# Attention without padded query and key products: a four-layer block kernel on one core

## Chip, cores, metric

The kernel runs on one core of a Trainium2 chip. A core has a matrix engine (TensorE; PE in the profile, its weight loads PEld), a vector engine (VectorE, DVE), a scalar engine (ScalarE, ACT), a general engine (GpSimd, POOL) and a queue engine (SyncE, SP), and 16 DMA engines that they share. Each engine works through its own instructions in order, and waits for others by semaphores. The matrix engine writes to PSUM, which has eight banks of 128 x 512 floats. DMAs here are issued from SP and from POOL. The metric is the device time of one launch, in microseconds.

## What is computed

Four layers stand behind each other on x of shape (4, 512, 288) in float32, with one condition vector per batch. Layers 0, 1 and 3 are transformer blocks with 16 heads of 18 features; layer 0's feed-forward part picks 2 of 4 experts for every token; layer 2 rotates x in a subspace of 64 dimensions. Cut down (n is a normalization, sh, sc and g come from the condition):

```python
h = n(x) * (1 + sc_msa) + sh_msa
q, k, v = split(h @ w_qkv + b_qkv)                 # 16 heads of 18 features
att = softmax(einsum("bhqd,bhkd->bhqk", q, k) * 18 ** -0.5)
x = x + g_msa * (einsum("bhqk,bhkd->bqhd", att, v) @ w_proj + b_proj)
h = n(x) * (1 + sc_mlp) + sh_mlp
x = x + g_mlp * (gelu(h @ w1 + b1) @ w2 + b2)      # layer 0: weighted sum over two experts
# layer 2: U = qr(P).Q; R = expm(skew(silu(cond) @ W.T + b)); x = x + ((x @ U) @ R - x @ U) @ U.T
```

## The kernel before

**Order.** The program is emitted in Python in the order in which the work is wanted, and a scheduler places the instructions of each engine; helpers pin the order where it matters. `mm` (L75) chains nearly all matmuls in program order. `take`, `beside_of` and `in_turn` (L95 to L105) keep, for an engine, the last instruction to which others are tied: `beside_of` puts an instruction behind it, `in_turn` also makes it the new last one.

**Stages.** In the profiled execution attention 0 runs to about 415 us, the experts to 931, attention 1 to 1303, the feed-forward part of layer 1 to 1485, the rotation and attention 3 to 1866, and layer 3's feed-forward part to the end. Side jobs (`tick`, L770) run through all of them: the Householder reflections of layer 2 (`reflections`, L577), the matrix exponential (`exponential`, L652), the modulation of the next layers (`modulation`, L320).

**Attention** (L776). A group r is four heads g of one batch b; there are 16 groups a layer. The four heads lie in the four quarters of the 128 partitions, each 18 features and 14 rows of padding, so that four products of 32 rows can run beside each other. `queries_and_keys(r)` (L829) projects the 128 padded rows of q and of k for 512 tokens: per side one product of the 32 features left over and two of 128 features, in halves of 256 tokens, into two `de` banks, from which ACT writes the tiles `qk0` and `qk1` with the bias (L856). The bias puts 1.0 into row 18 of every key head.

A group has 8 quads (`quad`, L888): k counts half a tile of 128 tokens, and a quad is two `row_max` (L862) and two `weight` (L875). `row_max` multiplies q by k to a 128 x 512 score tile, from which DVE takes the maximum of every row (L873). After the eighth quad `shift` (L913) transposes these maxima and subtracts them from the q tile, in row 18 of each head. So `weight`, which runs nine quads later with keys as rows, gets scores minus maximum, which ACT exponentiates (L885). `sums` (L898) multiplies the weights by the values, whose ones column gives the denominator; `collect` (L943) and `invert` (L964) move sums, denominators and reciprocals by DMAs on POOL and SP.

Between quads `work_off` (L1092) runs pieces of jobs by the letters of a table (L1042 to L1064): Q is the projection of group r + 1, A the transposed input of the next batch, X values or output projection, R the routing of the experts (L1717). Steps (L1039) stand at fixed quads: `invert(r - 2)` at k = 4, the sums at k = 1 and 5.

**PSUM.** One bank `av`, four `sc` (scores and hidden features), three `de` (all else), L64.

**Weights.** q and k weights come padded to 32 columns a head from the host (`_layout`, L2074): 288 x 1024 floats, loaded into `wqk` and `wqkr` (L241, L254). x of batches 1 to 3 is loaded tile by tile in 12 DMAs (L2025).

Of the kernel before, what the change touches and what calls it, by code (L numbers as in the profile page):

```python
# [16 lines left out]
P = 128  # L17
# [6 lines left out]
HC = P // D  # L24
OR = 64
# [3 lines left out]
E = 4  # L29
# [14 lines left out]
def kernel(ctx: ExitStack, tc: tile.TileContext, a: dict, out: bass.AP):  # L44
# [19 lines left out]
    banks = {"sc": 4, "de": 3}  # L64
# [4 lines left out]
    def misc(name):  # L69
        return bank("de", name)  # L70

# [21 lines left out]
    queues = {nc.sync: "SP", nc.scalar: "ACT"}  # L93
# [56 lines left out]


# [19 lines left out]
    def load_x(b):  # L171
        for t in range(NT):
            nc.sync.dma_start(x[:, b * NT + t, :], a["x"][b, t * P : (t + 1) * P, :])

# [62 lines left out]

    def attention_weights(l):

        w = {}  # L240
        w["qk"] = wt.tile([P, MC, 2 * NG * P], F32, tag="wqk", name=f"wqk{l}")  # L241
        w["qkr"] = wt.tile([2 * RR, NG * P], F32, tag="wqkr", name=f"wqkr{l}")
# [3 lines left out]
        w["bqk"] = wt.tile([P, 2 * NG], F32, tag="bqk", name=f"bqk{l}")  # L246
# [7 lines left out]
        def qk():  # L254
            load(w["bqk"], a[f"bqk{l}"])
            full_chunks(w["qk"], a[f"wqk{l}"])
# [6 lines left out]
        def qk_rest():  # L263
            for s in range(2):
                remainder(w["qkr"], a[f"wqk{l}"][:, :, s * NG * P : (s + 1) * NG * P], [s])

        def projection(g):
# [4 lines left out]
        return w, [  # L272
            qk,
            qk_rest,
# [41 lines left out]
    dram = ctx.enter_context(tc.tile_pool(name="dram", bufs=1, space=bass.MemoryType.DRAM))  # L316
# [3 lines left out]
    def modulation(l):  # L320
# [14 lines left out]
        def half(i):  # L335
# [25 lines left out]
            ps = misc(f"psada{l}_{i}")  # L361

            def products(ns):
                for kc in range(KC):
                    for n in ns:
                        q = (n + 1) % 3
                        nc.tensor.matmul(
                            ps[q * RR : (q + 1) * RR, 0:C],
                            lhsT=siluT[:, kc, :],
                            rhs=pieces[n][:, kc, :],  # L370
                            start=(kc == 0),
                            stop=(kc == KC - 1),
                        )

            def gated():
                nc.vector.tensor_add(gate[:, i, :], gate[:, i, :], ps[0:B, 0:C])
# [4 lines left out]
            if (l, i) in by_rows:  # L381
                for q, kept in ((1, shifts[l, i]), (2, scales[l, i])):
                    r = slice(q * RR, q * RR + B)
                    for k in range(KC):
                        row = a[f"adab{l}"][:, 3 * i + q - 1, k : k + 1].rearrange("p k -> k p")
                        to = rows[r, k * CP : (k + 1) * CP]
                        nc.gpsimd.dma_start(to, row.to_broadcast([B, CP]))
# [16 lines left out]
            for q in (1, 2):  # L404
                pm = misc(f"psmod{l}_{i}_{q}")
                r = slice(q * RR, (q + 1) * RR)
                for c in range(MC + 1):
                    nc.tensor.transpose(
# [8 lines left out]
            nc.vector.tensor_scalar_add(sc, sc, 1.0)  # L417
# [7 lines left out]
            if not whole:  # L425
                products([2])
                gated()
# [24 lines left out]
    def moments(name, b, eps):  # L452
# [6 lines left out]
        def step(t):  # L459
            beside_of("DVE", nc.vector.bn_stats(st[:, t, :], x[:, b * NT + t, :]))  # L460
            nc.vector.bn_aggr(mv[:, t, :], st[:, t, :])
            if t == NT - 1:
                nc.vector.tensor_scalar_add(ve, mv[:, :, 1], eps)
                ins = nc.gpsimd.tensor_tensor(rstd, ve, mhalf, ALU.pow)
                if name == "ln0_0_0":
                    beside_of("POOL", ins)
# [110 lines left out]
    def reflections():  # L577
# [11 lines left out]
        ps = bank("de", "psback")  # L589
# [156 lines left out]
    def rotation():  # L746
        yield from reflections()
        yield from subspace()
        for b in range(B):
            ps = bank("de", f"psue_{b}")  # L750
# [25 lines left out]
    def attention(l, w, mod, eps, feed, ticks, hT=None, then=None, also=()):  # L776
# [11 lines left out]
        with ExitStack() as es:  # L788
            pool = es.enter_context(tc.tile_pool(name=name, bufs=2))
            hTs, xns, vs, qks, raws, outs, gbs = {}, {}, {}, {}, {}, {}, {}  # L790
# [38 lines left out]
            def queries_and_keys(r):  # L829

                yield
                b, g = groups[r]
                ps = [bank("de", f"{name}psqk{r}_{s}") for s in range(2)]
                for s in range(2):
                    rows = slice(s * RR, (s + 1) * RR)
                    mm(
                        ps[s],
                        lhsT=w["qkr"][rows, g * P : (g + 1) * P],
                        rhs=hTs[b][rows, MC, :],
                        start=True,  # L840
                        stop=False,
                    )
                for s in range(2):
                    j = s * NG + g
                    for q in (slice(0, T // 2), slice(T // 2, T)):
                        for c in range(MC):
                            yield
                            mm(
                                ps[s][:, q],
                                lhsT=w["qk"][:, c, j * P : (j + 1) * P],  # L850
                                rhs=hTs[b][:, c, q],
                                start=False,
                                stop=(c == MC - 1 and q.stop == T),
                            )
                    t = pool.tile([P, T], F32, tag=f"qk{s}", name=f"{name}qk{r}_{s}", bufs=tags["qk0"])
                    nc.scalar.activation(t, ps[s], AF.Identity, bias=w["bqk"][:, j : j + 1])  # L856
                    qks[r, s] = t

            def heads_rows(i):
                return slice(i * DP, (i + 1) * DP)  # L860

            def row_max(r, t, i):  # L862
# [5 lines left out]
                    lhsT=qks[r, 0][heads_rows(i), t * P : (t + 1) * P],  # L868
                    rhs=qks[r, 1][heads_rows(i), :],
# [43 lines left out]
            def shift(r):  # L913
# [13 lines left out]
                take("DVE", nc.vector.tensor_sub(q, q, ps))  # L927
# [15 lines left out]
            def collect(r):  # L943
# [14 lines left out]
                for i, k, c, row in runs(g):  # L958
                    for j in range(k):
                        f = slice((i + j) * DP, (i + j) * DP + D)  # L960
                        for o, q in places(outs[b, "o"], c, row + j * D, D):
                            nc.gpsimd.dma_start(o, raw[f, q])
# [71 lines left out]
            def others(r):  # L1034
# [7 lines left out]
                pieces = {0: "QQ", 2: "QQQ", 3: "QQQ", 4: "XQX", 6: "XX", 7: "X"}  # L1042
# [18 lines left out]
                if g == 1 and b + 1 < B:  # L1061
                    jobs["A"] = activations(b + 1)
                    jobs["X"] = values(b + 1, 0)
                    pieces = {0: "QQA", 2: "QQQ", 3: "QQQ", 4: "QAA", 6: "XXX", 7: "XX"}  # L1064
# [32 lines left out]
            def places_of_first():  # L1097

                for f in range(NF):
                    q = f * feed.width % T  # L1100
                    if q == 0:
                        n = f * feed.width // T
                        tag = f"qk{n % 2}" if n < 4 else "p"
                        t = pool.tile([P, T], F32, tag=tag, name=f"{name}f{f}", bufs=tags[tag])
                    yield t[:, q : q + feed.width]

            tags = {"qk0": 3, "qk1": 3, "p": 10}

            loads = feed.loads(l)
            first = [queries_and_keys(0)]  # L1110
# [1049 lines left out]
```

## Time and profile before

| | |
|---|---|
| median of three runs | 2034.55 us (2031.51 to 2038.27) |
| the profiled execution | 2033.07 us |
| its span (first to last instruction) | 2031.4 us |
| mean granted clock of TensorE | 0.983 |
| DMA moved | 155.89 MB, mean 77 GB/s |
| row maxima, DVE, each of three layers | 256 of 0.68 to 0.69 us |
| exponentials, ACT, each layer | 256 of 0.596 us |

The profile is of one execution, whose own time lies 1.7 us above its span. A group of instructions is given as line, engine, operation, names of outputs and inputs, shapes, count, then busy time, mean duration in ns, and the idle time of the engine ahead of it with what ended that ("<-"). Every float32 matmul stands as two records. Matmuls overlap, so the mean duration of one is longer than the pace at which they follow each other; the pace is read from starts. "a1m" are the row maxima's scores of layer 1, "a1s" those of the weights, "a1psqk" the projection, "av" the sums, "e0h" and "e0o" the experts, "f1h" and "f1o" the feed-forward part of layer 1.

### The profile page before, as it was taken

Reading aid. Unit: us, or ns where it says so; the run is one execution under the profiler, and the core shown is the slowest. Engines: PE = TensorE matmul, PEld = TensorE weight load, DVE = VectorE, ACT = ScalarE, POOL = GpSimd, SP = SyncE. Lnnn points to the kernel's source line nnn. Section 1 sums busy time; section 2 is a strip of 40 time slices with the busy share of each in tenths; the row PEclk is TensorE's granted clock in tenths of the full one; section 3 lists DMA queues with packets and bytes.
Section 4 is the critical chain, followed back from the end, with each engine's and each line's share of the span. In section 5 each row is a group of like instructions: output and inputs, shape, how many; then the busy total and the mean of one; then the engine's idle time right before and its main releaser. Section 6 shows DMA issues by size and latency. Waiting matters only on the chain.

```text
span 2031.4 us, 29536 instructions
## 1 busy us (share of the span) xinstructions
PE 1957.2 (96%) x10932; PEld 1045.6 (51%) x10932; DVE 1074.3 (53%) x3103; ACT 765.4 (38%) x1409; POOL 569.2 (28%) x803
## 2 busy tenths in 40 slices
PE   7999999999999999999999999999999999999998
PEld 4434444466667777776434443456654344433565
DVE  5666777623454333446777877454255556554211
ACT  1545555333312232322555544421125455555220
POOL 3111221443434446651332122211401111213101
PEclk9989999899999999999999999999999899999999
DMA  7421111447655766751112111220000111111000
GB/s 152 119 52 20 23 33 34 106 121 222 180 155 163 223 191 206 220 183 30 45 42 43 33 39 40 47 69 19 21 1 10 28 29 35 28 27 23 18 16 22
DMA packets 95698, 155.89 MB, mean 77 GB/s; under 512 B 33571, under 2 KB 71310, under 8 KB 95554
## 3 DMA queue, kind: packets, MB, share of 16 engines
q0 software_dynamic: 28672, 89.90, 14.7%
q1 hardware_dynamic: 66770, 64.10, 13.8%
q8 instruction: 86, 1.41, 0.3%
q14 instruction: 58, 0.48, 0.1%
q10 hardware_dynamic: 112, 0.01, 0.0%
HBM read 125.29 MB, written 18.48 MB: 71 GB/s over the span
## 4 chain that ended last, share of the span: by engine, by line
PE 70%; DVE 7%; DMA 4%; POOL 1%; issue 1%; ACT 1%; SPq 0%; POOLq 0%; DVEq 0%; ACTq 0%
PE e0h L76 9%; PE e0o L76 8%; PE a3m L76 7%; PE a1m L76 6%; PE av L76 6%; PE a3psqk L76 4%; PE f1h L76 4%; PE f3h L76 4%; PE a1psqk L76 4%; PE f1o L76 3%; DVE max L873 3%; PE f3o L76 3%; DMA v<-pT 2%; DMA wr<-in_wrot 1%; PE a3psv L76 1%; PE a3pp L76 1%
## 5 line engine op out<-in xcount | busy, mean ns | idle before, releaser
L873 DVE TENSOR_REDUCE max<-a3m 128x1 f32<-128x512 f32 x256 | 164.6, 686 | 132.9 <-PE a3s L76 122.3
L76 PE MATMUL e0h<-e0hT,e0w 128*128 128x256 f32 (+1 forms) x1188 | 229.0, 404 | 4.9 <-DMA e0w<-w1c,wrow 4.2
L873 DVE TENSOR_REDUCE max<-a0m 128x1 f32<-128x512 f32 x256 | 165.3, 683 | 94.3 <-PE a0s L76 81.7
L873 DVE TENSOR_REDUCE max<-a1m 128x1 f32<-128x512 f32 x256 | 165.8, 684 | 75.0 <-PE a1s L76 68.4
L76 PE MATMUL e0o<-e0w,e0hm 128*128 128x288 f32 x756 | 201.6, 417 | 0.0
L76 PEld LDWEIGHTS e0h<-e0hT,e0w 128*128 128x128 f32 (+1 forms) x1188 | 166.2, 189 | 62.3 <-issue 37.1
L885 ACT ACTIVATE a0p<-a0s 128x512 f32<-128x512 f32 x256 | 140.2, 596 | 146.8 <-PE a0s L76 146.7
L885 ACT ACTIVATE a1p<-a1s 128x512 f32<-128x512 f32 x256 | 140.9, 596 | 142.4 <-PE a1s L76 142.1
L885 ACT ACTIVATE a3p<-a3s 128x512 f32<-128x512 f32 x256 | 140.0, 596 | 139.2 <-PE a3s L76 139.1
L76 PE MATMUL a1m<-a1qk,a1qk 32*128 32x512 f32 x512 | 159.2, 647 | 8.0 <-DVE max L873 6.9
L76 PE MATMUL a0m<-a0qk,a0qk 32*128 32x512 f32 x512 | 159.4, 647 | 6.4 <-DVE max L873 5.3
L76 PEld LDWEIGHTS e0o<-e0w,e0hm 128*128 128x128 f32 x756 | 141.9, 192 | 42.5 <-issue 4.0
L76 PE MATMUL a0s<-a0qk,a0qk 32*128 32x512 f32 x512 | 160.4, 655 | 1.3 <-DVE max L873 1.3
L76 PE MATMUL a1s<-a1qk,a1qk 32*128 32x512 f32 x512 | 159.8, 647 | 0.2 <-DVE u L547 0.2
L76 PE MATMUL a3m<-a3qk,a3qk 32*128 32x512 f32 x512 | 152.1, 647 | 6.8 <-DVE max L873 5.5
L76 PE MATMUL a3s<-a3qk,a3qk 32*128 32x512 f32 x512 | 153.5, 647 | 0.3 <-DVE a3qk L927 0.3
L1279 ACT ACTIVATE e0hm<-e0h,e0w 128x256 f32<-128x256 f32 x189 | 89.5, 473 | 166.7 <-PE e0h L76 166.7
L607 POOL TENSOR_TENSOR nrm<-n,phalf 64x1 f32<-64x1 f32 (+31 forms) x64 | 36.6, 573 | 297.9 <-DVE n L604 294.1
L1813 ACT COPY e0r<-e0o 128x288 f32<-128x288 f32 x44 | 17.5, 398 | 184.1 <-PE e0o L76 176.4
L76 PEld LDWEIGHTS a1m<-a1qk,a1qk 32*128 32x128 f32 x512 | 47.4, 184 | 72.8 <-DVE max L873 44.1
L76 PEld LDWEIGHTS a0m<-a0qk,a0qk 32*128 32x128 f32 x512 | 47.4, 185 | 67.9 <-DVE max L873 38.8
L76 PE MATMUL f1h<-f1hT,w 128*128 128x512 f32 (+1 forms) x216 | 80.8, 614 | 0.4 <-ACT f1hT L502 0.4
(465 smaller groups left out, 3270.0 us busy)
## 6 DMA issues: line engine op xcount, KB each, us to landing
eo<-e0r SPq DMA_DIRECT2D x44, 144.0 KB
ada<-in_ada SPq DMA_DIRECT2D x18, 324.0 KB
wr<-in_wrot SPq DMA_DIRECT2D x16, 288.0 KB
g<-gates SPq DMA_DIRECT2D x24, 144.0 KB
w1c<-in_w SPq DMA_DIRECT2D x20, 144.0 KB
w<-in_w SPq DMA_DIRECT2D x6, 432.0 KB
x<-in_x SPq DMA_DIRECT2D x16, 144.0 KB
w1c<-in_w SPq DMA_DIRECT2D x8, 288.0 KB
```

The lines of the kernel that those rows point to most:

```text
L76: ins = nc.tensor.matmul(*args, **kwargs).ins
L607: in_turn("POOL", nc.gpsimd.tensor_tensor(nrm, n2, phalf[0:n], ALU.pow))
L873: take("DVE", nc.vector.tensor_reduce(m[:, t, i, D : D + 1], ps, AX.X, ALU.max))
L885: take("ACT", nc.scalar.activation(p, ps, AF.Exp, scale=D**-0.5))
L1279: nc.scalar.activation(self.hms[i][f], ps[r][:, 0 : self.width], func, bias=b1(f)),
L1813: take("ACT", nc.scalar.copy(y, ps))
```

## The change

Queries and keys are projected from weights without padding. The 576 columns of q and k are ordered by group (four heads of q, four of k) and cut into chunks of seven heads, 126 columns; a batch has five chunks, and a group needs one more of them than the group before it (the first of a batch needs two). A chunk goes into two `de` banks, one for each half of the tokens, from which ACT writes a tile `u` with the bias. Eight DMAs a group then copy the heads, 18 rows each, to their places in the padded tiles: those of q on SP, those of k on POOL, both in fixed order. Three pairs of padded tiles are made once for a layer; q's padding is zeros and k's is the ones row, which the host's bias gave before. `row_max` now uses 18 rows, since row 18 of a q tile still holds the maxima of three groups ago; the shift clears it by a mask.

Of the eight banks five are now `sc` and two `de`; the contractions of the feed-forward parts, the side jobs inside an attention and the rotation's products take `sc` banks. A quad issues its weights ahead of its row maxima. The tables of pieces are written anew, and the values of the first two tiles are computed ahead of the first quad.

Layer 0's padded weights are loaded into the place of x's batches 1 to 3 and copied narrow by ACT; after that x is loaded in one DMA for each batch. For layers 1 and 3 twelve DMAs in attention 0 copy the weights without padding from DRAM to DRAM.

```diff
-    banks = {"sc": 4, "de": 3}
+    banks = {"sc": 5, "de": 2}
...
+    def aside_bank(name):
+        return bank("sc" if inside[0] else "de", name)
...
+    flag = cst.tile([P, 1], F32, tag="flag", name="flag")
+    nc.vector.tensor_reduce(flag, ident[:, D::DP], AX.X, ALU.add)
+    mask = cst.tile([P, 1], F32, tag="mask", name="mask")
+    nc.vector.tensor_scalar(mask, flag, -1.0, 1.0, ALU.mult, ALU.add)
...
+    def load_whole(b):
+        to = x[:, b * NT : (b + 1) * NT, :]
+        nc.sync.dma_start(to, a["x"][b].rearrange("(t p) c -> p t c", p=P))
...
+    def compacting():
...
+        def step(l, k, n):
+            to = compact[l][n, :, k, :]
+            src = a[f"wqk{l}"][:, k, n * NG * P : (n + 1) * NG * P]
+            src = src.rearrange("p (h e) -> p h e", e=DP)[:, :, 0:D]
+            beside_of("SP", nc.sync.dma_start(to, src))
...
+        def wide():
...
+            full_chunks(full, a[f"wqk{l}"])
+            rest = t[:, MC * n : (MC + 1) * n]
+            remainder(rest, a[f"wqk{l}"], range(2))
...
+            def narrow():
+                for m in range(MC + 1):
...
+                    for s in range(2):
+                        beside_of("ACT", nc.scalar.copy(o[s], heads(i)[s][:, :, :, 0:D]))
...
             def queries_and_keys(r):
...
+                for c in range(g + 1 if g else 0, g + 2):
+                    yield
+                    m = min(UC, 2 * C - c * UC)
+                    cols = slice(c * UC, c * UC + m)
+                    ps = [bank("de", f"{name}psqk{r}_{c}_{k}") for k in range(2)]
+                    tokens = [slice(k * T // 2, (k + 1) * T // 2) for k in range(2)]
...
+                    for k in range(2):
+                        product(k, MC, slice(k * RR, (k + 1) * RR))
+                    u = us[b, c] = pool.tile([P, T], F32, tag="u", name=f"{name}u{r}_{c}")
+                    for k in range(2):
+                        for n in range(MC):
                             yield
+                            product(k, n, slice(0, P))
+                        nc.scalar.activation(
+                            u[0:m, tokens[k]],
+                            ps[k][0:m, 0 : T // 2],
+                            AF.Identity,
+                            bias=w["bu"][0:m, c : c + 1],
+                        )
+
+                for i in range(GH):
+                    for s, queue in ((0, nc.sync), (1, nc.gpsimd)):
+                        c, row = divmod((2 * g + s) * GH + i, HC)
+                        o = qks[r, s][i * DP : i * DP + D, :]
+                        ins = queue.dma_start(o, us[b, c][row * D : (row + 1) * D, :])
+                        in_turn("POOL" if s else "SP", ins)
...
-                take("DVE", nc.vector.tensor_sub(q, q, ps))
+                take(
+                    "DVE",
+                    nc.vector.scalar_tensor_tensor(q, q, mask, ps, ALU.mult, ALU.subtract),
+                )
...
-                pieces = {0: "QQ", 2: "QQQ", 3: "QQQ", 4: "XQX", 6: "XX", 7: "X"}
+                pieces = {0: "QQ", 2: "QQ", 3: "Q", 4: "XX", 6: "XX", 7: "X"}
+                if g == NG - 1:
+                    pieces = {0: "QQQ", 2: "QQ", 3: "QQQ", 4: "QQ", 6: "XXX", 7: "XX"}
...
+            def padding(r):
+                beside_of("DVE", nc.vector.memset(qks[r, 0], 0.0))
+                beside_of("DVE", nc.vector.tensor_copy(qks[r, 1], flag.to_broadcast([P, T])))
...
-            first = [queries_and_keys(0)]
+            first = [queries_and_keys(0), values(0, 0)]
...
-            for t, pieces in enumerate(("QQQQ", "QQQQQ", "XXXXX", "YYYYY")):
+            for t, pieces in enumerate(("QQ", "QQQ", "XX", "XXX")):
                 quad([(row_max, 0, 2 * t), (row_max, 0, 2 * t + 1)])
+                if t == 0:
+                    padding(1)
+                    padding(2)
...
-                    quad([(row_max, r, k)] + lagging(8 * r + k - 9))
+                    quad(lagging(8 * r + k - 9) + [(row_max, r, k)])
...
-                ps = bank("de", f"{self.name}o{i}_{t}")
+                ps = bank("sc", f"{self.name}o{i}_{t}")
```

## The prediction

> **What bounds the kernel now.** I read the page first, then the busy time by stretches, the groups of instructions kept apart by shape, the chain of waits by line, the order of instructions in time inside attention, and the DMA issues. A group below means four heads of one batch, as in the code; it holds eight quads, k = 0 to 7.
>
> ```profile
> span 2031.4 us, 29536 instructions
> PE 1957.2 (96%) x10932; PEld 1045.6 (51%) x10932; DVE 1074.3 (53%) x3103; ACT 765.4 (38%) x1409; POOL 569.2 (28%) x803
> PE 70%; DVE 7%; DMA 4%; POOL 1%; issue 1%; ACT 1%; SPq 0%; POOLq 0%; DVEq 0%; ACTq 0%
> ...
> 954.00:1282.00 328.00, 317.72 (x1920) 131.53 (x1918) 249.69 (x617) 164.24 (x288) 78.56 (x120) 0.99 0.18 38
> 1535.00:1836.00 301.00, 293.81 (x1817) 120.33 (x1818) 180.16 (x323) 153.67 (x273) 55.32 (x94) 0.98 0.13 27
> ```
>
> In the two stretches (inside the attentions of layers 1 and 3) the columns are length, then busy PE, PEld, DVE, ACT and POOL, the granted PE clock, the DMA engines' busy share and GB/s: PE is busy 97% of each. The chain of waits gives DVE 7%; by line, 3.5% (71 us) of the span is the row maximum, L873. So PE bounds attention, except where a matmul waits for a score bank. The order in time shows both, in one group of layer 1 without other jobs:
>
> ```profile
> 1025.22 0.69 PE L76 MATMUL a1m<-a1qk,a1qk 32*128 32x512 f32 x1
> ...
> 1026.29 1.56 PE L76 MATMUL a1psqk<-a1hT,wqk 128*128 128x256 f32 x6
> 1027.78 0.69 PE L76 MATMUL a1m<-a1qk,a1qk 32*128 32x512 f32 x1
> ...
> 1035.77 0.69 PE L76 MATMUL a1m<-a1qk,a1qk 32*128 32x512 f32 x1
> ...
> 1037.67 0.69 PE L76 MATMUL a1m<-a1qk,a1qk 32*128 32x512 f32 x1 [0.76 <-DVE max L873]
> ...
> 1040.84 0.33 PE L76 MATMUL a1sh<-ident,max 128*128 128x128 f32 x1 [0.97 <-DVE max L873]
> ...
> 1042.06 1.03 PE L76 MATMUL a1psqk<-a1hT,wqkr 32*128 32x512 f32 x4
> 1043.02 0.70 PE L76 MATMUL a1psqk<-a1hT,wqk 128*128 128x256 f32 x2
> ```
>
> A quad that starts at 1025.22 gives way at 1026.29 (1.07 us), six query and key matmuls follow until 1027.78 (0.249 us each), and the next quad starts at once: PE-bound. Between 1035.77 and 1037.67 there is nothing to do, and the quad waits 0.76 us for a maximum. The whole group took 1041.10 - 1019.75 = 21.35 us.
>
> **The change: projection.** Per layer the 128x256 matmuls fall from 256 records to 4 batches x 5 chunks x 4 products x 2 records = 160. The 32-row ones go from 64 of 512 columns to 80 of 256.
>
> ```profile
> L76 PE MATMUL a3psqk<-a3hT,wqk 128*128 128x256 f32 x256 | 74.2, 418 | 0.0
> L76 PE MATMUL a1psqk<-a1hT,wqk 128*128 128x256 f32 x256 | 71.0, 403 | 0.0
> L76 PE MATMUL a3psqk<-a3hT,wqkr 32*128 32x512 f32 x64 | 18.8, 645 | 0.0
> ```
>
> At the pace seen (0.249 us; four 32-row ones from 1042.06 to 1043.02, so 0.24 each and 0.12 at half width) a layer saves 96 x 0.249 = 23.9 and 64 x 0.24 - 80 x 0.12 = 5.8, together 29.7 us, or 1.85 us for each of 16 groups. Over the 45 groups r = 1 to 15 that is 83 us.
>
> The evictions of a batch become 10 of 128x256 (473 ns in the nearest ACT row) where 8 of 688 ns stood: 0.8 us less on ACT, which isn't the bound: 0. The masked subtraction costs DVE what a 128x288 one of its kind does over a plain sum (494 against 456 ns), so 0.06 us x 48, behind PE's next quad: 0.
>
> **The change: score banks.** Now a quad needs, bank by bank, what the quad before it released; its second maximum is released last (start + 1.1 + 0.07 + 2 x 0.65 = 2.5 us). With five banks and weights first, the third bank awaits the first maximum (1.85) and the fourth the second exponential (1.15 + 1.1 = 2.3, from a pair of 1.08 on ACT). The second maximum drops out. But less filler lies between quads: 1.0 us (one pair of 32-row products, one product) at k = 0 and 2, 0.5 at k = 3, against 1.5. Chaining eight quads by hand, each starting when PE is free and ending no earlier than its start's predecessor + 2.3 + 1.07, a plain group takes 18.75 us instead of 21.35 (-2.6). One that projects two chunks (next group opens a batch; three a layer) gets 20.6 instead of some 22 (-1.4). That is 36 x 2.6 + 9 x 1.4 = 106 us. The bounds: the PE sum alone, 83, and 106. I take 95, since DVE also runs other things in these gaps.
>
> A rule of the Trainium skill speaks against this: "TensorEngine Tiling (Array Packing)", Performance Considerations, says that row tiling speeds TensorE up but not the emptying of PSUM, which may then set the pace. The 0.76 us wait above agrees with it; by the rule alone the saving would shrink towards the first rival's.
>
> **The change: copies.** Every group adds eight DMAs of 18 x 2 KB, four on SP and four on POOL.
>
> ```profile
> 105.93 0.61 SPq L970 DMA_DIRECT2D a0one<-a0den  x1
> 108.11 1.63 SPq L974 DMA_DIRECT2D a0or<-a0one  x2
> ```
> ```profile
> 345.98 2.05 POOL L962 DMA_DIRECT2D a0oo<-a0raw  x4 [4.22 <-ACT a0raw L910]
> a1oo<-a1raw POOLq DMA_DIRECT2D x56, 36.0 KB, 1.9
> ```
>
> POOL issues such copies (same size) in 0.5 us each and they land 1.9 us later; on SP a small one takes 0.6, and the second line starts 2.2 us after the first, which it awaits. The projection of a plain group ends at k = 3, so the copies leave at about 10.1 us of the group and land from 12.3 to 14.1; they are needed from 18.75 on. Cover: 4.6 us, so cost 0 (0 to 4.6 late would still cost 0). For a two-chunk group they are issued after k = 4, and on SP behind the inversion's DMAs of two groups back (one 0.6, its landing, two more 1.6): they leave at 17.6, land 19.8 to 21.6, and are needed from 20.6, each head half a quad or more after the last. Cover under 1 us: I take 0.5 x 9 = 5 us (0 to 15). Queued behind the copies are the denominators' DMAs on SP, needed groups later, and on POOL the square roots of the reflections and of the normalization, for which DVE waits; these come 2 us later, one or two quads before their use: nothing, at most 1 us x 12. WAR on the padded tiles costs nothing: three sets rotate and the last reader is one quad into the group.
>
> **Compaction.** Twelve DRAM to DRAM copies of 1536 runs of 72 B for layers 1 and 3 go onto SP in attention 0.
>
> ```profile
> q1 hardware_dynamic: 66770, 64.10, 13.8%
> ```
>
> The columns are packets, MB and the share of 16 engines. A packet of this queue takes 0.138 x 16 x 2031 / 66770 = 67 ns on average; 96 per engine are 6.4 us a copy. In the built order three sets of query copies stand directly behind one: I take 8 us (0 to 20, if all stand in the way for longer).
>
> "DMA: Bandwidth & Descriptors", Specifications, wants 512 B per transfer and has read-modify-write below; no row here shows 72 B copies. Were a packet doubled by this, these 8 us would be 15.
>
> **Starts.** Layer 0's weights must be narrowed by six ACT copies, of which the nearest row (128x288 copy, 398 ns) gives 2.4 us, ahead of the three hT evictions (2.1 us), while projection now starts at 21.1 us on a DMA (0.94 us wait). I take +3.3 (0 to 6). In each layer the first row maxima await the copies and the values of two tiles drawn ahead (2.6 us), +3.5, while the four opening steps lose projection and the same values: 16.7 to 14.2, held there by four maxima (2.5 us) each and four 0.5 us memsets. +1 a layer: together +6 (0 to 14).
>
> **Two banks for the rest.** The experts' transposes (22 items, three tiles of 0.3 us on two banks) now wait for a 377 ns copy: 18 more close pairs x 0.3 = 5; the normalization's, 11 x 0.3 = 3; contractions move to the score banks, -2. +6 (0 to 15).
>
> **Sum.** -95 + 5 + 8 + 6 + 6 = -70 against the profiled execution's own 2033.07 (span 2031.4): 1963. The median of the runs shown is 1.5 us above that execution, so 1964. All bounds low: -106; all high: -83 + 15 + 12 + 20 + 14 + 15 = -7, so 1928 to 2027.
>
> **Rivals.** *Evictions take over.* Filling the empty gaps with 3.3 us of output projection made a group 21.98 instead of 21.35 us: PE work was free there. If five banks don't shorten the wait (2.29 us a quad on average with 1 us of filler, four banks chained likewise), a group saves 1.5, 67 us less 25 to 30 of costs: 1995. Against it: the projection is cut at k = 0, 2, 3, whose 2.56 us periods have no wait at all.
>
> *Copies come late; slower.* One mechanism: the first row maximum of a group waits for the fourth copy on SP or POOL, both in order and shared with weights, gates, gathers. It decides from a landing 4.6 us later than I have it, plus 70 / 45 = 1.6 us: 6.2 us. At 8 us late the price is 3.4 x 45 = 153 us, so 2034 + 153 - 70 = 2117; at 7 us, 2072. For it: SP also carries 432 KB weight loads in eight pieces at k = 6. Against: the DMA engines are busy 0.13 to 0.18 of these stretches, and the copies stand ahead of the inversion in plain groups.
>
> *Waits vanish more fully.* The 71 us of row maximum in the chain mostly go too: 83 + 40 - 15 of costs, 1926.
>
> **Chances.** Forecast (1930 to 1980) 0.58; evictions 0.20; fuller 0.08; late copies 0.11; the rest, 0.03, gives no change. A measurement here tells 0.3% (6 us) from none. Faster 0.86, same 0.03, slower 0.11. The range, 1922 to 2025, holds the first two and part of the third.
>
> **What would show it.** Right: the 128x256 projection at 160 records a layer and near 45 us; groups of 18.5 to 19.5 us; no matmul of line a?m idle on a DMA; "DVE max" smaller in the chain. Wrong: idle time of a?m or a?s released by a?qk copies (late copies), groups of 20 us and waits on ACT's exponential or the maximum at k = 2 to 4 (evictions), a start of attention 0 later than 36 us, waits of e0xt on its copy above 10 us.

## The result and the profile after

The changed kernel takes 2146.19 us (median of four runs, 2134.4 to 2154.53) against 2033.3 us (2031.51 to 2038.27) of the kernel before in the same session: 1.055 times as long, 95% interval 1.048 to 1.061. The forecast was 1964 us, and its range ended at 2025.

The page of the profiled execution (2154.46 us): span; PE's busy time, share and instructions; the chain of waits by engine; the granted TensorE clock in 40 slices of 54 us, in tenths, where 9 stands for 0.9 and more.

```profile
span 2152.8 us, 30929 instructions
PE 2024.2 (94%) x10692; PEld 1061.1 (49%) x10692; DVE 1086.1 (50%) x3123; ACT 753.7 (35%) x1439; POOL 673.9 (31%) x1006
PE 64%; DVE 6%; DMA 6%; POOL 2%; issue 2%; ACT 1%; SPq 0%; POOLq 0%; DVEq 0%; ACTq 0%
PEclk9867999889998799999899999999999999989999
```

PE has fewer instructions than before and is busy 67 us longer: it runs slower. The mean granted clock over the span is 0.929, against 0.983. The trace has only two values of it, full and half: half clock lasts 307 us in 30 stretches after, 68 us in 10 before. Half of the time for which PE was busy in such stretches is lost to the clock: 132 us after, 32 before. (In the rest of them PE was waiting, and a wait is not longer at half clock.) PE is not busy for 128.6 us (2152.8 - 2024.2) where it was 74.2. So of the 121 us between the spans 100 are slower matmuls and 54 are longer waits, and only 33 us of work saved stand against them.

The same stretches inside attentions 1 and 3 as in the prediction, each moved with the start of its attention (length, then busy PE, PEld, DVE, ACT, POOL; clock, DMA share, GB/s), and four groups of the projection by shape:

```profile
1052.00:1380.00 328.00, 313.65 (x1792) 128.46 (x1790) 239.75 (x586) 154.94 (x289) 102.61 (x172) 0.93 0.22 50
1645.00:1946.00 301.00, 294.23 (x1711) 120.20 (x1709) 175.19 (x311) 145.00 (x273) 77.09 (x140) 0.93 0.18 40
```
```profile
L82 PE MATMUL a1psqk<-a1hT,wqk 128*126 128x256 f32 x128 | 40.1, 436 | 0.0
L82 PE MATMUL a1psqk<-a1hT,wqk 128*72 128x256 f32 x32 | 9.6, 401 | 0.0
L82 PE MATMUL a1psqk<-a1hT,wqkr 32*126 32x256 f32 x64 | 14.7, 464 | 0.0
L82 PE MATMUL a1psqk<-a1hT,wqkr 32*72 32x256 f32 x16 | 2.4, 374 | 0.0
```

The 32-row products of the kernel before, in the same attention:

```profile
L76 PE MATMUL a1psqk<-a1hT,wqkr 32*128 32x512 f32 x64 | 17.0, 594 | 0.0
```

The 128-row part of the projection did shrink as forecast: 160 records and 49.7 us where 256 records and 71.0 us stood. The 32-row products did not: 17.1 us for 17.0. And the stretches run at a clock of 0.93 instead of 0.98 to 0.99. By stages (first matmul of one to first matmul of the next) the 121 us fall into attention 0 and what stands ahead of it (61 us), the experts (33), attention 1 (17), its feed-forward part and the rotation (1), and attention 3 and the end (9).

Where a new batch begins (a boundary, below; there are three in each attention), the timeline of attention 1 shows the mechanism (start, duration, engine or queue, line, output and input, count; in brackets PE's idle time ahead of the instruction and who ended it):

```profile
1106.79 0.60 SPq L1063 DMA_DIRECT2D a1one<-a1den  x1
1109.45 1.64 SPq L1067 DMA_DIRECT2D a1or<-a1one  x2
1111.20 6.63 SPq L946 DMA_DIRECT2D a1qk<-a1u  x4
1117.93 0.71 SPq L621 DMA_DIRECT2D v<-pT  x1
1118.08 1.19 PE L82 MATMUL a1m<-a1qk,a1qk 18*128 18x512 f32 x1 [2.67 <-DMA a1qk<-a1u]
```

The four query copies were ready at 1106.8, when POOL issued the key copies. On SP they stood behind the inversion of two groups back, whose second step awaits the landing of its first, so they began at 1111.2, and their issue took 6.6 us; elsewhere in attentions 1 and 3 four such copies take 3.0 to 3.3. The matmul that needs them came at 1118.1, at half the clock (1.19 us for a record of 0.69). PE waits for copies at the nine boundaries and nowhere else: 0.3 to 9.3 us each, 23.7 us in all.

The 6.6 us recur at eight of the nine boundaries (6.58 to 6.76), and the first copy alone takes 4.3 of them. It is no matter of copies: of the DMAs issued directly behind the two of the inversion's second step, 10 of 17 took 4.3 us here and 7 of 16 in the kernel before, the others 1.7 to 1.8. There it was, among others, a weight load:

```profile
1103.47 1.68 SPq L974 DMA_DIRECT2D a1or<-a1one  x2
1105.20 4.27 SPq L178 DMA_DIRECT2D w<-in_w  x1
```

The clock fell as the long wait began, not after it. The trace has half clock from 1115.6 to 1125.8, and PE's wait of 2.67 us began at 1115.4. In the 3.4 us ahead of the fall PE had been idle for 0.9 us, in short waits:

```profile
1112.20:1115.60 3.40, 2.50 (x10) 0.74 (x6) 2.49 (x5) 0.69 (x2) 2.16 (x3) 1.00 0.23 25
1115.60:1125.80 10.20, 7.72 (x28) 3.22 (x32) 3.11 (x7) 1.93 (x4) 2.23 (x3) 0.50 0.39 106
```

In attention 0 the twelve compaction copies add to this. Two windows of 10 us, then SP's queue, then the two waits of PE:

```profile
120.00:130.00 10.00, 4.35 (x12) 1.68 (x12) 4.50 (x12) 1.19 (x2) 1.57 (x2) 0.50 0.17 16
130.00:140.00 10.00, 3.80 (x8) 1.18 (x6) 2.01 (x5) 1.19 (x2) 0.00 (x0) 0.50 0.32 41
```
```profile
101.34 5.78 SPq L266 DMA_DIRECT2D wqkc<-in_wqk  x2
...
111.37 5.09 SPq L1050 DMA_DIRECT2D a0den<-a0raw  x1
...
129.18 1.65 SPq L1067 DMA_DIRECT2D a0or<-a0one  x2
130.88 4.29 SPq L266 DMA_DIRECT2D wqkc<-in_wqk  x1
135.27 3.42 SPq L946 DMA_DIRECT2D a0qk<-a0u  x4
```
```profile
125.65 1.22 PE L82 MATMUL a0s<-a0qk,a0qk 32*128 32x512 f32 x1 [9.22 <-DVE max L963]
143.05 1.19 PE L82 MATMUL a0m<-a0qk,a0qk 18*128 18x512 f32 x1 [9.25 <-DMA a0qk<-a0u]
```

Three of the twelve compaction copies take SP 2.8 to 5.1 us, the others 0.6 to 1.3. The 4.29 us above is again the place directly behind the inversion's second step. The denominators' DMA behind the first copies took 5.1 us. Their reciprocal waits 12.3 us at the head of DVE's order, ahead of the row maximum that PE awaits. Half clock lasts from 118.9 to 153.0. A third place, which the prediction did not name at all, is the loads of layer 0's shift and scale biases, tied into POOL's order by the change:

```profile
188.28 3.79 POOL L465 DMA_DIRECT2D rows<-in_adab  x4 [6.80 <-DMA a0oo<-a0raw]
197.10 0.45 DVE L466 SCALAR_TENSOR_TENSOR rows<-psada,rows 4x288 f32<-4x288 f32 x1 [11.73 <-DMA rows<-in_adab]
198.33 1.22 PE L82 MATMUL a0m<-a0qk,a0qk 18*128 18x512 f32 x1 [8.58 <-DVE max L963]
```

Before, the same loads went out at 12.9 us and DVE never waited for them.

### The profile page after: what moved, and what is told of

Same layout as the page of the kernel before. It is cut to its first block, busy times and chain, and to the rows that moved or that the text cites. A ratio compares the mean times of both kernels' runs of the same rounds, so it can differ in the third digit from the quotient of the medians.

```text
span 2152.8 us, 30929 instructions
## 1 busy us (share of the span) xinstructions
PE 2024.2 (94%) x10692; PEld 1061.1 (49%) x10692; DVE 1086.1 (50%) x3123; ACT 753.7 (35%) x1439; POOL 673.9 (31%) x1006
## 4 chain that ended last, share of the span: by engine, by line
PE 64%; DVE 6%; DMA 6%; POOL 2%; issue 2%; ACT 1%; SPq 0%; POOLq 0%; DVEq 0%; ACTq 0%
PE e0h L82 8%; PE e0o L82 7%; PE av L82 6%; PE a3s L82 5%; PE a1s L82 5%; PE f1h L82 4%; PE f3h L82 4%; PE f1o L82 3%; PE f3o L82 3%; DVE max L963 3%; PE a3psqk L82 3%; PE a1psqk L82 2%; PE a3m L82 2%; PE a1m L82 1%; DMA wr<-in_wrot 1%
## 5 line engine op out<-in xcount | busy, mean ns | idle before, releaser
L82 PE MATMUL e0o<-e0w,e0hm 128*128 128x288 f32 x756 | 209.5, 428 | 0.0
L82 PE MATMUL a0m<-a0qk,a0qk 18*128 18x512 f32 x512 | 186.0, 721 | 21.6 <-DMA a0qk<-a0u 11.3
L82 PE MATMUL a0s<-a0qk,a0qk 32*128 32x512 f32 x512 | 178.5, 713 | 13.5 <-DVE max L963 13.5
L82 PE MATMUL a1m<-a1qk,a1qk 18*128 18x512 f32 x512 | 182.3, 690 | 8.3 <-DMA a1qk<-a1u 8.3
L82 PE MATMUL a3m<-a3qk,a3qk 18*128 18x512 f32 x512 | 172.8, 677 | 4.0 <-DMA a3qk<-a3u 4.0
L82 PE MATMUL a1s<-a1qk,a1qk 32*128 32x512 f32 x512 | 170.9, 671 | 1.7 <-DVE max L963 1.3
L82 PE MATMUL a3s<-a3qk,a3qk 32*128 32x512 f32 x512 | 163.6, 669 | 0.3 <-DVE a3qk L1019 0.3
L1055 POOL DMA_DIRECT2D a0oo<-a0raw x72 | 36.6, 516 | 193.3 <-ACT a0raw L1000 193.3
L1055 POOL DMA_DIRECT2D a3oo<-a3raw x72 | 36.1, 509 | 176.5 <-ACT a3raw L1000 173.8
L82 PEld LDWEIGHTS a0s<-a0qk,a0qk 32*128 32x128 f32 x512 | 50.9, 203 | 78.7 <-DVE max L963 41.8
```

The lines of the kernel that those rows point to most:

```text
L82: ins = nc.tensor.matmul(*args, **kwargs).ins
L1055: take("POOL", nc.gpsimd.dma_start(o, raw[f, q]))
```

## The experiments

Times are medians, compared with the changed kernel's 2146.19 us unless another is named; the kernel before took 2032 to 2038 us beside them. Single runs of one kernel lie mostly within 15 us of its median, the farthest 20. Groups are measured from the start of one shift (`a1sh`) to the next, so that the wait of a new batch falls into groups 4, 8 and 12. (The expectations of the first runs cut them at the first quad instead; their 46.9 and 44.4 us lie in groups 3 to 5 here.)

**No compaction.** `compact[l]` becomes two views of the padded weights, and `step` returns without a DMA.

```diff
-            compact[l] = dram.tile([2, CP, KC, C], F32, tag=f"wqkc{l}", name=f"wqkc{l}")
+            src = a[f"wqk{l}"]
+            compact[l] = [src[:, :, n * NG * P : n * NG * P + C] for n in range(2)]
...
-            beside_of("SP", nc.sync.dma_start(to, src))
+            return
```

> The changed kernel without its twelve compaction copies: the loads of layers 1 and 3 take the first 288 columns of each padded half instead, so queries and keys of these layers have wrong values, and every size stays. Theory 'short packets': groups 3 and 4 of attention 0 took 46.9 and 44.4 us because copies of 72-byte runs filled the SP queue and the DMA engines, so that denominators and query copies landed late; without them these groups fall to 21 to 28 us and the time from 2146 to 2090 - 2110. Rival 'inversion ahead': they are late because the query copies stand behind the inversion on SP, as in the other attentions; then the two groups stay above 35 us and the time above 2130.

2115.36 us (2112.22 to 2135.38), 31 less. Groups 3 and 4 of attention 0 fell from 31.7 and 35.1 to 19.9 and 25.7 us. Group 5 kept 42.2: that is the bias loads. The compaction's cost is shown, at a smaller size than expected; how much of it is SP's issue and how much the DMA engines was not separated.

**Inversion behind the copies.**

```diff
-                    steps[4].append(lambda: invert(r - 2))
+                    steps[6 if g == NG - 1 else 4].append(lambda: invert(r - 2))
```

> The changed kernel with the inversion moved from step 4 to step 6 in the last group of a batch, so that on SP the query copies of a two-chunk group stand ahead of the inversion's DMAs. Theory 'inversion ahead': the first groups of a batch, now 26 to 31 us in attentions 1 and 3, fall to 21 - 23 (about 6 us for each of nine, some of it returned clock), and the time to 2080 - 2105. Rival 'late from the start': the second chunk is evicted at the end of step 4 and the keys' copies on POOL are no earlier, so the boundary keeps most of its wait, gain under 20 us, 2125 - 2146.

2092.0 us (2083.94 to 2099.09), 54 less. The groups at the nine boundaries are 1.2 to 9.5 us shorter, 6 on average and 53 together, and PE waits for no copy any more. SP's queue at the first boundary of attention 1, with the copies now 10 us ahead of the inversion (group 4 went from 28.8 to 24.2 us):

```profile
1073.81 3.22 SPq L946 DMA_DIRECT2D a1qk<-a1u  x4
...
1083.68 0.65 SPq L1063 DMA_DIRECT2D a1one<-a1den  x1
...
1087.53 4.34 SPq L193 DMA_DIRECT2D w<-in_w  x1
```

Groups 8 and 12 of attention 1 went from 29.0 and 25.1 to 20.1 us. The copies needed no faster transfer, only their place in the queue: with the same sizes they are issued in 3.2 us, and the 4.3 us fall on a weight load, as in the kernel before. In the traces PE's idle time fell by 29 us and the loss to the clock by 19.

**Both.**

> Both edits (no compaction, wrong values in layers 1 and 3; inversion at step 6). If the two costs are separate, their gains add: some 45 + 55 us, 2035 - 2065. If one wait hides behind the other, the sum is smaller than the parts, above 2070. If projection and banks brought the 95 us that the prediction gave them, and only these two places took them back, it would be 1960 - 1980.

2070.35 us (2067.37 to 2073.34): 76 of the 85 us that the parts gave. The costs are nearly separate. And with both gone the kernel is still slower than before: these two places do not account for the 95 us, which would have given 1960 to 1980.

This trace shows a further loss, in the experts. PE's transposes, then four stretches of 6 us:

```profile
637.52 0.44 PE L82 MATMUL e0xt<-ident,e0xs 128*128 128x128 f32 x2 [0.46 <-ACT e0hT L1912]
638.42 1.03 PE L82 MATMUL e0xt<-ident,e0xs 128*32 128x128 f32 x16 [0.46 <-ACT e0hT L1912]
```
```profile
632.00:638.00 6.00, 5.50 (x47) 4.42 (x45) 2.32 (x6) 2.01 (x6) 0.40 (x1) 1.00 0.99 341
638.00:644.00 6.00, 5.58 (x31) 3.28 (x32) 2.37 (x11) 0.74 (x2) 1.56 (x2) 0.54 0.09 20
644.00:650.00 6.00, 6.00 (x24) 4.09 (x24) 0.84 (x2) 0.00 (x0) 1.90 (x2) 0.50 0.42 123
656.00:662.00 6.00, 6.00 (x22) 4.04 (x23) 1.02 (x5) 0.59 (x2) 0.00 (x0) 0.50 0.66 176
```

After two waits of 0.46 us for a copy that frees one of two banks, among narrow products and transposes, the clock is 0.5 for some 24 us, with PE busy all the while: about 12 us lost. That the two waits bring the fall is the order seen, not shown by a run. The same stretch lasts 23.9 us in the two kernels above as well and 41.0 us in the changed one (682 to 723 us); the next kernel, with three `de` banks, has not got it.

**Old banks, new projection.**

```diff
-    banks = {"sc": 5, "de": 2}
+    banks = {"sc": 4, "de": 3}
...
-                    quad(lagging(8 * r + k - 9) + [(row_max, r, k)])
+                    quad([(row_max, r, k)] + lagging(8 * r + k - 9))
```

(`aside_bank` and the contractions take `de` again.)

> The changed kernel with four and three banks and the row maximum first in a quad again, as in the kernel before; the other matmuls back on the banks that they had. Theory 'TensorE bound': most groups carry values or an output projection, and their TensorE work alone is 19.5 us, so banks and order move little, and the time is 2140 - 2165. Rival 'banks pay as predicted': without them each of 45 groups waits 0.3 us or more again, over 2165. Second rival 'two banks are too few': experts and normalization gain, under 2135.

2137.38 us (2133.55 to 2138.59): 9 less, within what runs differ by. In the changed kernel as it stands banks and order bring nothing: plain groups are some 0.5 us shorter (19.5 for 20.0), the experts 22 us longer (560 against 538). Half of the 22 is one execution's clock, since the experts took 548 to 550 in the three kernels above, which have the same banks.

**Bias loads free again.**

```diff
-                        beside_of("POOL", nc.gpsimd.dma_start(to, row.to_broadcast([B, CP])))
+                        nc.gpsimd.dma_start(to, row.to_broadcast([B, CP]))
```

> The changed kernel with one word of the change undone: the six loads of layer 0's shift and scale biases (rows<-in_adab on POOL) are free in the queue again, as in the kernel before, where they went out at 12.9 us; in the changed kernel they stand in program order, go out at 179 to 188 us and DVE waits 11.7 us for them ahead of a row maximum. Theory 'late biases': the sixth group of attention 0 (48 us) falls to 25 - 30 and the time by 15 - 25 us, 2120 - 2132. Rival 'late anyway': the group waits for the short-packet copies' backlog, and the gain stays under 8 us, 2138 or more.

2134.08 us (2130.54 to 2146.62), 12 less, between the two. Group 5 of attention 0 fell from 48.4 to 35.0, but attention 0 began at 42.1 instead of 33.8 us: the loads now went out ahead of the first query copies, which landed late.

**All causes at once**, with new and with old banks. The compaction gives way to padded loads, which ACT narrows in six copies a layer; the experts' third transposed tile takes an `sc` bank.

```diff
-                ps = misc(f"{self.name}xt{i}_{c}")
+                ps = bank("sc" if c == MC else "de", f"{self.name}xt{i}_{c}")
```

> Every cause found so far taken out at once, with the right results: inversion at step 6 in the last group of a batch; the bias loads free; no compaction (layers 1 and 3 load padded pieces and ACT narrows them, 6 small copies each); in the experts the third transposed tile of an item on a score bank. If the causes are complete apart from starts: e3_both's 2070, less 20 for the biases and 15 - 20 for the experts' transposes with the halved clock after them, 2025 - 2040. If the clock in the experts halves for another reason, 2045 - 2060.

> As e7_fix, but with four and three banks, the row maximum first, and the other matmuls on the banks that they had before. This prices banks and order alone, with no stall in the way. Theory 'TensorE bound': the groups lose 0.3 us each without them, 45 x 0.3 = 14, and the experts gain what the transposes lose in e7_fix: e8 within 15 us of e7_fix. The prediction's step, 95 less the 83 of the projection and up, would make e8_fix43 slower by 12 - 95 us than e7_fix.

2054.96 us (2040.21 to 2070.4) and 2077.78 us (2070.98 to 2079.69). The first is 91 us off the changed kernel and 17 above the one before (ratio 1.009, interval 1.005 to 1.013); the upper of its two forecasts held. With the stalls gone, banks, order and the moved tile are worth 23 us, more than the 15 of the first theory and at the low end of what the prediction's step allowed. Three `de` banks did not make the experts shorter here: 547 us, against 537 with two and the moved tile.

**Bias loads ahead of their step** (as the first of these, with the loads moved up in POOL's order).

> As e7_fix, but the six bias loads of layer 0 stand in order on POOL again, ahead of the three weight loads of their step instead of behind their product. In e7_fix, free, they went out at 20.3 us and the first query copies behind them landed late: the first score matmul of attention 0 started at 42.9 us against 33.8 in the changed kernel. If that is all, the start returns to 34 us and the sixth group of attention 0 stays at 23 - 27: 7 - 10 us off e7_fix's 2055, 2043 - 2049. If they are still late for DVE, the sixth group is over 30 us and nothing is won.

2058.45 us (2050.47 to 2062.14): nothing won. Attention 0 began at 35.2 us instead of 42.9, but its groups 4 and 5 took 29.5 and 26.8 instead of 22.2 and 22.8.

**Useless matmuls.** The last trace still had a mean clock of 0.947. In attentions 1 and 3 the groups without values or projection were the slow ones.

```diff
+            def filler(r, steps):
+                ...
+                    mm(ps[:, 0 : T // 2], lhsT=w["v"][:, k % MC, 0:P], rhs=..., ...)
...
+                if 0 < r < n and "X" not in jobs and (l > 0 or r < 13):
+                    jobs["X"] = filler(r, 4)
+                if r == n - 1 and l > 0:
+                    jobs["Q"] = filler(r, 8)
```

> As e9_rows2, with useless matmuls added: four of 128x256 in each group that has no values or output projection (groups 3 and 4 of every attention, 13 and 14 of attentions 1 and 3), and eight in the last group of attentions 1 and 3, where the next projection is missing; nothing reads them. They are some 1 to 2 us of TensorE work each, 16 us in all (10 groups x 1.0 + 2 x 2.0 = 14). Theory 'clock': in e7_fix the granted clock is 0.58 to 0.9 in the last groups of attentions 1 and 3 because TensorE pauses between quads; the filled pauses keep it at 1, groups 14 and 15 of attention 1 fall from 24.7 and 26.2 to 20 - 22, and the time is the same as e9_rows2's or up to 15 us below it in spite of the work. Rival 'plain work': the clock there has other reasons, and the time is 10 - 16 us above e9_rows2's.

2039.04 us (2024.48 to 2047.69): 19 less for some 24 us of work that nothing reads. (A float32 matmul is two records: 112 of them at the pace of 0.22 us that a row of such matmuls shows below. The expectation priced one each.) It equals the kernel before (ratio 1.000, 0.997 to 1.003). Groups 14 and 15 of attention 1, first without the filler (the kernel with all causes out), then with it; the columns as above:

```profile
1256.00:1281.00 25.00, 24.23 (x115) 8.08 (x115) 17.62 (x43) 10.24 (x20) 3.99 (x8) 0.80 0.26 60
1281.00:1307.00 26.00, 25.26 (x112) 9.03 (x112) 19.64 (x56) 9.55 (x18) 5.42 (x8) 0.74 0.10 23
```
```profile
1255.00:1277.00 22.00, 21.67 (x119) 7.52 (x117) 16.93 (x42) 9.71 (x19) 4.00 (x8) 0.92 0.29 67
1277.00:1299.00 22.00, 21.77 (x130) 9.36 (x129) 19.70 (x56) 9.81 (x19) 5.43 (x8) 1.00 0.13 28
```

The clock is back at 0.92 and 1.00, and the two groups take 22.5 and 21.9 us instead of 24.7 and 26.2.

**Banks and order**, on the kernel before (its pieces of projection moved so that two banks suffice).

> The kernel before with the changed kernel's banks and order alone: five and two banks, weights first in a quad, the other matmuls on the same banks as in the changed kernel, pieces of projection, activations and routing moved so that two banks suffice; projection, tiles and copies as before. The prediction's chain gave a group without other work 0.76 us of wait at one quad and less elsewhere: 45 groups x 0.3 to 0.5 = 14 to 22 us faster, 2012 - 2022. Theory 'TensorE bound, and experts pay': groups gain some 10 us in sum, the experts lose 10 to 20 us at transposes and halved clock, 2030 - 2045.

2099.72 us (2095.62 to 2107.61): 62 us slower than the kernel before, which neither theory had. Groups 5 to 12 of attention 1, most of which carry values or an output projection, took 22.5 to 24.5 us instead of 20.9 to 23.2. That fits the projection of that kernel, which holds both `de` banks from its first product to its last eviction, so that the other jobs wait for it; it was not tried apart from the moved pieces. Groups without such work (3, 13 and 14) took 20.5, 20.4 and 21.0 instead of 21.4, 21.0 and 22.0, and in attention 3 only 0.1 to 0.2 us less than before. So 0.1 to 1.0 us a group is what five banks and the order gave where nothing else is in the way.

**Filler in the openings** (twelve matmuls ahead of the first quad, three behind each of four).

> As e10_fill, with more useless matmuls (128x256, nothing reads them) in the openings of the three attentions: twelve (some 3 us) while the first query copies land, and three (0.75 us) behind each of the four opening quads. In e10_fill the granted clock is 0.5 for 20 to 25 us from the opening of attentions 0, 1 and 3 on. Theory 'clock': the openings run at 0.8 and above, each attention's first two groups lose 4 to 8 us, and the time falls by 10 to 20 us to 2019 - 2029, below the kernel before. Rival: the copies, not the clock, set the openings; each then costs up to 6 us of added work, 2039 - 2055.

2048.26 us (2036.22 to 2063.64), 9 more than without: a miss. The mean clock rose from 0.961 to 0.974, but the added work stood on the path. The twelve matmuls are 24 records and took 5.3 us, not the 3 that were priced:

```profile
960.48 5.34 PE L82 MATMUL a1more<-a1hT,wv 128*128 128x256 f32 x24
```

PE had not been waiting there: without them it goes from the values to the first score at once, so each of the three attentions came to its first scores 5 us later. The first two groups of an attention together won only 0.5 to 2.4 us.

**Order alone.**

> As e10_fill, with the row maximum first in a quad again and all else as it is: what weights first is worth by itself with five banks. By the prediction's chain the second maximum is the bank released last, so with the maximum first a quad could start up to 0.65 us earlier or wait 0.45 us longer for the exponential; it counts on weights first. Expected: 2039 - 2055 if weights first helps in pauses of groups (up to 0.3 us x 45); 2030 - 2039 if the order is worth nothing or costs.

2068.01 us (2061.68 to 2072.13), 29 more than the same kernel with weights first, and more than expected: with five banks the order is worth about as much as banks, order and moved tile together.

Profiled executions side by side, in us: PE's idle time, half of the time that PE was busy at half clock ("lost"), and the span without that loss. The last column is an estimate of what a full clock would give if all else stayed.

```
                             span    clock   idle    lost    span - lost
before                      2031.4   0.983    74.2    32.2   1999
changed                     2152.8   0.929   128.6   132.3   2020
no compaction               2113.3   0.936   101.0   124.1   1989
inversion behind            2093.5   0.940   100.0   113.1   1980
both                        2071.6   0.946    90.1   103.2   1968
old banks, new projection   2135.1   0.937   135.7   116.6   2018
bias loads free             2128.8   0.936   127.2   117.3   2012
all causes out              2052.6   0.953    86.3    90.2   1962
the same, old banks         2076.9   0.952   100.2    91.8   1985
all out, biases earlier     2058.9   0.947    80.8   103.6   1955
with useless matmuls        2038.5   0.961    75.1    72.7   1966
the same, old order         2062.4   0.961    70.5    74.3   1988
filler in the openings      2043.9   0.974    75.4    49.6   1994
banks and order, old proj.  2093.9   0.975   101.8    49.2   2045
```

Without the loss, the kernels "all causes out", "biases earlier" and "with useless matmuls" are 33 to 44 us better than the one before. On the wall they are not, because the lower clock takes it back.

## Why the prediction was wrong

**Projection: right but for one term.** 160 records of 128x256 a layer; 40.1 + 9.6 us in attention 1 where "near 45" was forecast. The 32-row products were to save 5.8 us a layer at half their width and saved none: 14.7 + 2.4 us for 17.0. So busy time fell by 21 us in this layer, not by 29.7.

**Copies: the step that failed first.** The prediction saw that the two-chunk group's query copies stand behind the inversion's DMAs, with "cover under 1 us". Then it took 0.5 us for each of nine, bounds 0 to 15 us. Measured, the place in the queue costs 54 us, 6 us a boundary. It priced the inversion by its own 0.6 and 1.6 us and left out the 4.3 us for which the next DMA behind it was issued, a row of the trace before (1105.20, above). And it priced lateness alone: moving the copies ahead took 29 us of idle time and 19 us of lost clock off. In plain groups the cover held: no wait on a copy shows there.

**Compaction: mis-sized.** 8 us (0 to 20) became 31. A packet was priced alone. What the trace shows is SP's in-order issue, three copies of 2.8 to 5.1 us (one of them behind the inversion again), and the denominators behind them, for which DVE waits ahead of row maxima.

**A moved instruction not seen.** The six bias loads, 12 us by the experiment and some 20 at their place (group 5 of attention 0 took 42.5 us with both edits and 22.8 with all causes out). They are one word of the whole change, which the excerpt of it above does not show, and stand in no step of the sum.

**Banks and order: mis-sized.** -95 was taken, PE's 83 included. The best kernel here shows what is there without stalls: over groups 2 to 14 it is 0.8 us a group faster than before in attention 1 (20.95 against 21.75) and 1.35 in attention 3 (20.2 against 21.5), but 0.55 in attention 0 (21.8 against 22.35), so some 40 us over 45 groups. The model was one group without other work, 21.35 us, expected at 18.75; most groups carry values or an output projection. Groups of one chunk and values (2, 6, 10) came to 19.5 to 20.5 us, those with two chunks and an output projection (7, 11) stayed at 21.5 to 22.7.

**Two banks for the rest: mis-sized.** +6 (0 to 15) in the experts and elsewhere. The experts alone were 33 us longer than before (560 for 527). With three banks they took 538 and 547 us, in the other kernels with two 537 to 550, so what the banks have in the 33 is not settled; 27 us of the 560 are lost to the clock, 8 of the 527. **Starts: at the upper bound.** Attention 0 began 3.9 us later (3.3 forecast), and the first two groups of the three attentions took 5.2, 2.9 and 2.0 us more: 14 in all, of +6 (0 to 14).

**No term for the clock.** The working showed the clock column (0.99, 0.98) and drew nothing from it, and priced every wait by its own length. "TensorE: Matmul & The Clock Gate", HAM oscillation, in the Trainium skill speaks of this: matmuls that wait for data let the clock fall to half, and the next ones start slow. The trace agrees that half clock follows waits, but they were shorter than the 3.4 us that the page gives as its window: 0.9 us of idle time in 3.4 at the boundary shown above, twice 0.46 us in the experts. All fourteen traces say the same. Half clock comes in multiples of 3.4 us. Taken in steps of that length, a step at full clock in which PE was busy for less than half the time was followed by half clock in 91 of 123 cases, one in which it was busy for nine tenths or more in 76 of 6778. That is a count, not a cause; the useless matmuls are the test: more work, 19 us less.

The rival "Copies come late; slower" named the right mechanism and the right sign, but asked for copies 6 us later in all 45 groups. They were late in nine, which is 54 of the 113 us that the kernel lost against the one before; without them it is still slower. "Evictions take over" has its number: groups 2, 6 and 10 of attentions 1 and 3 saved 1.4 to 1.6 us where it said 1.5 and the forecast 2.6. That evictions are the reason is not shown.

What stays open: why the clock falls in the experts even where the third tile has a bank of its own (0.5 from 625 to 642 us with useless matmuls in the attentions; there PE waited 1.27 us for a step of the matrix exponential just before, but 1.57 us at the same place in the kernel with all causes out brought no such fall). Why the DMA behind the inversion's second step takes 4.3 us to issue is open too. It is not its own kind, since query copies, compaction copies and weight loads all show it, and no weight load stood in SP's queue in the 20 us ahead of 1111.2.

## What to carry to other kernels

A small DMA costs what stands ahead of it in its queue, not what it moves: before adding one to an in-order queue, list what is behind which wait there, and put what the next matmul needs ahead of chains that await their own landings. Where TensorE is the bound, taking matmuls away can make pauses, as here, and a pause is priced at its length plus the slow matmuls after it: compare PE's idle time and its time at half clock before believing a saving. Price useless work by its records in a trace too. When tables, queues and ties are rewritten together, follow every instruction that changed its place, also those that are not the point of the change.

## What was not expected of the hardware

Useless matmuls made the kernel faster: 2058.45 to 2039.04 us; the clock of two groups was 0.80 and 0.74 with all causes out and 0.92 and 1.00 with them. The DMA issued directly behind the inversion's second step often took SP 4.3 us, be it a query copy (eight of nine boundaries) or a weight load (1105.20 before, 1087.53 with the inversion behind). The clock stayed at 0.5 for some 24 us while PE was 100% busy with products (644 to 662 us in the experts of the kernel without both stalls), and for 41 us in the changed kernel (682 to 723 us). Loads of 1.5 KB in single floats landed 9.8 us after issue (10.7 before), and while DRAM to DRAM copies in 72-byte runs were under way the DMA engines were 84% busy at 58 GB/s (110 to 120 us in attention 0; 15% at 21 GB/s without the compaction).
